# A graph attention layer's aggregation product in seven half-size products instead of eight

## The chip, the cores and the metric

The kernel runs on one core of a Trainium2 chip. The metric is the device time of one execution in microseconds. The times before and after are medians of several runs. The kernel is written so that the order of the instructions on TensorE (PE), VectorE (DVE), ScalarE (ACT) and the SyncE queue that issues the DMAs (SP) is the order in which the program states them, engine by engine; semaphores are set between the engines wherever one needs another's result.

## The reference

For each of 32 batches, with n = 512 nodes and d = 512 features, all in f32:

```
layer 0:  q, k, v = x Wq' + bq, x Wk' + bk, x Wv' + bv        (8 heads of 64)
          a = softmax(q k' / 8 + log(max(adj, 1e-8)))
          y = layer_norm(x + concat(a v) Wo' + bo) * gamma + beta
layer 1:  p = y fc_w' + fc_b
          m = (p q_w + q_b) + (p k_w + k_b)' + (1 - adj) * -1e9
          e = softmax(leaky_relu(m))
          out = e p + y
```

In layer 1 the kernel does not form p. With n the normalised rows ahead of gamma and beta, it computes e n first (with e not yet divided by its row sums), then multiplies by fc with gamma folded in, divides by the row sums and adds gamma n and a constant row, called cc, that holds beta and the bias of the projection. The product e n, stored transposed in a tile named zT, is what is changed.

## The kernel before

A batch b is worked in four slots, one for each pair of heads, p = 0 to 3; I call them the first to the fourth slot. Each slot computes the scores of one pair of heads (`score`, L814, with the exponential at L819), multiplies them by the adjacency (`factors`, L827), adds up their rows (`sums`, L837 and L840) and multiplies by v for the pair before (`values`, L852). Around this, the slots carry work of other batches, written out by hand:

- The first slot of batch b has e n of batch b - 2 (`z`, which calls `z_units`, products at L310, copies out of PSUM at L452). The transposes of e (`eT`, L535) and of the adjacency (`turn_a`, L557) come ahead of it on VectorE; after it come gamma n and the constant row (`residual`, L443 and L444), the reciprocal of the row sums (L437) and `divided`, which checks and inverts softmax sums, stores them with one small DMA (L895) and loads them spread out with two (L898) into a tile R.
- The second slot has the output projection of layer 0 of batch b - 1 (`seven_wo`), its sums on VectorE at L740 and its adds at L744, then the statistics of the layer norm (`stats_units`). It begins with the loads of n and of the next x.
- The third slot normalises (`normalise_units`), takes dot products with the k vector (L376), and does the last projection of batch b - 2 (`seven_out`, called from `layer1_rows`): `z_sums` makes two sums of quarters of zT, one of them in a tile z3; the products are at L205, the sums between them at L761, the adds of the results at L767. The transposes of the next x are among them.
- The fourth slot has v of the next batch (`seven_v`) and the softmax of layer 1 of batch b - 1.

In every slot the next pair's q and k are made by `seven_qk` (L604), as four units; the second, third and fourth end with ScalarE or VectorE work, the adds of the last two at L634, L638 and L639.

All the functions whose names begin with `seven` use Winograd's form of Strassen's method: a 512x512x512 product is cut into quarters, and seven products of quarters, with sums of quarters made on VectorE ahead of them and adds of results behind them, do the work of eight. A product of quarters is four matmuls of 128x128 weights with 256 columns. e n is made in the plain way: 16 matmuls with 512 columns. A matmul of f32 is two records in the trace, so this is 32 records, and a product of quarters 8.

The tiles that matter: n (a batch's normalised rows), eP (transposed e), L1 (holds e's rows early, zT later), yb (gamma n + cc, later the output rows), R (two halves of 512 columns). A pool of three PSUM banks, `ps_m`, serves e n, the W_o and v projections and the last projection.

Of the kernel before, what the change touches and what calls it, by code (L numbers as in the profile page):

```python
# [9 lines left out]
FP = mybir.dt.float32  # L10
# [20 lines left out]
def kernel(  # L31
# [19 lines left out]
    k_b: bass.AP,  # L51
    out: bass.AP,
):

# [381 lines left out]

    def residual(s, cs=slice(0, 4)):

        def over(row):
            return row.unsqueeze(1).to_broadcast([P, cs.stop - cs.start, D])
        nc.vector.tensor_mul(s["yb"][:, cs, :], s["n"][:, cs, :], over(K["gamma"]))  # L443
        nc.vector.tensor_add(s["yb"][:, cs, :], s["yb"][:, cs, :], over(K["cc"]))  # L444

    def z_units(s, psum, name):

# [30 lines left out]
    def fast(ctx):  # L478
# [18 lines left out]

        cT = act.tile([P, NC, N], FP, name="cT")
        L1 = act.tile([P, NC, N], FP, name="L1")

        def load_a(b, kcs):

# [52 lines left out]
        def turn_a(kcs):  # L555
            for kc in kcs:
                nc.vector.transpose(cT[:, kc, :], cT[:, kc, :])  # L557
# [33 lines left out]
        def seven_qk(b, p):  # L591

            qk_tiles(b, p)
            s = S[b]
            q, k = s["qT", p], s["kT", p]
            bq, bk = K["bq"][:, p : p + 1], K["bk"][:, p : p + 1]
            wq, wk, W = K["wq"], K["wk"], K["qk_s"]
            left = {1: wq[:, :KH], 2: wq[:, KH:], 3: W[:, 2], 4: wk[:, KH:],
                    5: W[:, 0], 6: W[:, 1], 7: wk[:, :KH]}
            ps = {}  # L600

            def mul(i, to, first):
                for c in range(KH):
                    nc.tensor.matmul(  # L604
                        to, left[i][:, c, ts(p, P)], s["B"][i][:, c, :],
                        start=(first and c == 0), stop=(c == KH - 1),
                        skip_group_check=True,
                    )

            def banks():  # L610
                f = [ps_s.tile([P, 2, N], FP, tag="s", name=f"f_{b}_{p}_{i}") for i in range(2)]
                for i, name in enumerate("acbd"):
                    ps[name] = f[i % 2][:, i // 2, :H]

            def unit0():
                banks()
                mul(1, ps["a"], True)
                mul(5, ps["c"], True)  # L620
                nc.scalar.copy(ps["b"], ps["a"])  # L621
                nc.scalar.activation(k[:, H:], ps["c"], AF.Identity, bias=bk)

            def unit1():
                mul(6, ps["a"], False)
                mul(2, ps["b"], False)
                nc.scalar.activation(q[:, H:], ps["a"], AF.Identity, bias=bq)  # L627
                nc.scalar.activation(q[:, :H], ps["b"], AF.Identity, bias=bq)

            def unit2():  # L630
                mul(4, ps["d"], True)
                mul(3, ps["c"], False)
                nc.scalar.activation(k[:, :H], ps["d"], AF.Identity, bias=bk, scale=-1.0)  # L633
                nc.vector.tensor_add(q[:, H:], ps["c"], q[:, H:])  # L634

            def unit3():
                mul(7, ps["a"], False)
                nc.vector.tensor_add(k[:, H:], ps["a"], k[:, H:])  # L638
                nc.vector.tensor_add(k[:, :H], ps["a"], k[:, :H])  # L639
            return [unit0, unit1, unit2, unit3]  # L640

        def seven_v(b):

# [105 lines left out]
        def seven_out(b):  # L749

            s = S[b]
            yb, zT, r = s["yb"], s["zT"], s["r"]
            tiles = {
                f"{i + 1}{j + 1}": zT[:, ts(j, KH), ts(i, H)] for i in range(2) for j in range(2)
            }
            tiles["s3"] = s["z3"]
            data = {i: [t[:, c, :] for c in range(KH)] for i, t in tiles.items()}
            ps = {}

            def sub(i, x, y):  # L760
                nc.vector.tensor_sub(tiles[i], tiles[x], tiles[y])  # L761

            def add(i, j, name):
                for c in range(KH):
                    row = i * KH + c
                    o = yb[:, row, ts(j, H)]
                    nc.vector.scalar_tensor_tensor(  # L767
                        o, ps[name][:, c, :], r[:, row : row + 1], o, ALU.mult, ALU.add
                    )

            def store(i):
                nc.sync.dma_start(
                    out=out[b][ts(i, KH * P), :].rearrange("(c p) d -> p c d", p=P),
                    in_=yb[:, ts(i, KH), :],
                )

            def unit0(unit):
                ps.update(zip("bac", long_banks(f"o{b}")()))
                unit(True)
            muls, adds = seven_rows(data, sub, K["fc_s"], K["fc"], lambda n: ps[n], add, True)  # L780
            muls[0] = lambda unit=muls[0]: unit0(unit)
            adds[2].insert(1, lambda: store(0))
            adds[3].append(lambda: store(1))
            return muls, adds

        def z_sums(b):

            s = S[b]
            zT = s["zT"]
            s["z3"] = act.tile([P, KH, H], FP, tag="z3", name=f"z3_{b}")  # L790
            a11, a21, a22 = zT[:, :KH, :H], zT[:, :KH, H:], zT[:, KH:, H:]
            nc.vector.tensor_sub(s["z3"], a11, a21)
            nc.vector.tensor_add(a21, a21, a22)

        def long_banks(b):
# [159 lines left out]
        def z(b):  # L955
            s = S[b]
            s["zT"] = L1
            return z_units(s, ps_m, b)

        def eT(b):  # L960
            s = S[b]
            if b >= B - 2:
                t = io.tile([P, NC, N], FP, tag="x", name=f"eT_{b}")
                s["eT"] = t.rearrange("p t (c n) -> p t c n", c=NC)
                return transpose_units(s["e"], t, ps_m, nc.scalar.copy, f"e_{b}")
            s["eT"] = s["eP"].rearrange("p c (t n) -> p t c n", t=NC)
            return transposes(s["eP"], s["eP"])
# [64 lines left out]
        def slot(b, p):  # L1032
# [38 lines left out]
            if p == 0 and last >= 0:  # L1071
                if b >= 2:
                    run(eT(b - 2))
                turn_a((2, 3))
                divide(last, 2)
            factors(b, p, 1)
            if p == 3 and last >= 0:
                divided(b, 0)
            if p == 2:
# [4 lines left out]
                next_qk = seven_qk(b, p + 1)  # L1084
            else:
                next_qk = seven_qk(nxt, 0)
            if p == 0:
                sums(b, p, 0)
                if b == 0:
                    run(combine(K["wv"], K["v_s"])[:1] + combine_qk()[:1])  # L1090
                run(next_qk)
                units = z(b - 2) if b >= 2 else [lambda: spread(ps_o)] if b == 1 else first_v[2:]
                run(units)
                if b == 1:
                    combine_right(K["fc"], K["fc_s"])
                if b == 0:
                    run(combine(K["wv"], K["v_s"])[1:])
                if b >= 2:
                    rest_of_layer1(b - 2)
                if last >= 0:  # L1100
                    divided(last, 2)
            if p == 1:
                sums(b, 0, 1)
                if last < 0:
                    sums(b, p, 1)
                    run(next_qk)
                    bias()
                else:
                    for i in range(3):
                        wos[i + 1]()  # L1110
                        run(wo_adds[i])
                        if i == 1:
                            sums(b, p, 1)
                        next_qk[i]()
                    next_qk[3]()
                    wos[4]()
                    run(wo_adds[3])
                    run(stats_units(S[last], small, last))
            if p == 2:
                if b == 0:  # L1120
                    combine_right(K["wo"], K["wo_s"])
                    run(next_qk)
                    run(xT(nxt))
                    sums(b, p, 0)
                    offset()
                    divided(b, 0)
                else:
                    return layer1_rows(b, next_qk, norm[1:])
            if p == 3:
                load_a(nxt, (2, 3))  # L1130
                vs = seven_v(nxt)
                vs[0]()
                run(soft[1:2])
                next_qk[0]()
                vs[1]()
                next_qk[1]()
                run(soft[2:])
                sums(b, 2, 1)
                vs[2]()
                next_qk[2]()  # L1140
                next_qk[3]()
                vs[3]()
                turn_a((0, 1))
                sums(b, p, 0)
                sums(b, p, 1)
# [299 lines left out]
```

## Time and profile before

| what | value |
|---|---|
| median of 3 runs | 3474.84 us (3474.70 to 3476.26) |
| the profiled execution's own time | 3475.4 us |
| its span in the profile | 3473.5 us |
| TensorE busy | 3451.6 us, 99% of the span |
| VectorE busy | 2813.1 us, 81% |
| ScalarE busy | 1375.9 us, 40% |
| granted TensorE clock | 0.999 |
| DMA | 250.81 MB, mean 72 GB/s |

The profile has a page of totals and groups, and the trace behind it can be asked for a stretch of time. "Busy" counts the time in which an engine had an instruction running. TensorE's records overlap[...], so the distance from start to start tells more than the length. A row of a timeline gives the start, the length, the engine, the line in the source, the operation, the tile written and those read, the shape, how many instructions were merged into the row, and in brackets how long the engine had been idle before it and what it had waited for. A row of the waits gives who waited for whom, the total, the number of times and the longest.

### The profile page before, as it was taken

Reading aid. Unit: us, or ns where it says so; the run is one execution under the profiler, and the core shown is the slowest. Engines: PE = TensorE matmul, PEld = TensorE weight load, DVE = VectorE, ACT = ScalarE, POOL = GpSimd, SP = SyncE. Lnnn points to the kernel's source line nnn. Section 1 sums busy time; section 2 is a strip of 40 time slices with the busy share of each in tenths; the row PEclk is TensorE's granted clock in tenths of the full one; section 3 lists DMA queues with packets and bytes.
Section 4 is the critical chain, followed back from the end, with each engine's and each line's share of the span. In section 5 each row is a group of like instructions: output and inputs, shape, how many; then the busy total and the mean of one; then the engine's idle time right before and its main releaser. Section 6 shows DMA issues by size and latency. Waiting matters only on the chain.

```text
span 3473.5 us, 40744 instructions
## 1 busy us (share of the span) xinstructions
PE 3451.6 (99%) x14530; PEld 2193.0 (63%) x14530; DVE 2813.1 (81%) x4911; ACT 1375.9 (40%) x2338; POOL 1.0 (0%) x9
## 2 busy tenths in 40 slices
PE   9999999999999999999999999999999999999998
PEld 3666666666666666666666666676666666666654
DVE  5888888788887888788888878888788878888875
ACT  3343443434433444434334333443344343434432
POOL 0000000000000000000000000000000000000000
PEclk9999999999999999999999999999999999999999
DMA  4244243343333442433424334333344243343420
GB/s 116 41 74 89 59 87 66 56 89 78 70 71 57 82 89 59 80 68 62 89 63 84 65 56 89 80 68 73 59 77 89 59 82 65 62 89 65 82 74 31
DMA packets 880025, 250.81 MB, mean 72 GB/s; under 512 B 806732, under 2 KB 806988, under 8 KB 879816
## 3 DMA queue, kind: packets, MB, share of 16 engines
q1 hardware_dynamic: 879816, 248.15, 36.5%
q8 instruction: 116, 1.90, 0.2%
q14 instruction: 93, 0.76, 0.1%
HBM read 181.93 MB, written 34.65 MB: 62 GB/s over the span
## 4 chain that ended last, share of the span: by engine, by line
PE 97%; DVE 2%; DMA 1%; ACT 0%; issue 0%; SPq 0%; DVEq 0%; ACTq 0%
PE f L604 22%; PE sc L814 14%; PE po L852 13%; PE pz L310 12%; PE pw_a L205 6%; PE pv_a L205 5%; PE pw_o_a L205 4%; PE pw_c L205 3%; PE pv_b L205 3%; PE pv_c L205 3%; PE pw_o_b L205 3%; PE pw_o_c L205 3%; PE ps L869 2%; PE pw_b L205 2%; PE pg L310 1%; PE pk L310 0%
## 5 line engine op out<-in xcount | busy, mean ns | idle before, releaser
L827 DVE SCALAR_TENSOR_TENSOR at<-cT,at 128x1024 f32<-128x1024 f32 x512 | 601.1, 1215 | 224.0 <-ACT at L819 220.4
L819 ACT ACTIVATE at<-sc 128x1024 f32<-128x1024 f32 x512 | 496.6, 1022 | 604.2 <-PE sc L814 603.0
L814 PE MATMUL sc<-qT,kT 64*128 64x512 f32 x2048 | 508.8, 615 | 2.2 <-DVE kT L639 2.2
L852 PE MATMUL po<-at,v 128*64 128x512 f32 x2048 | 467.8, 599 | 0.0
L310 PE MATMUL pz<-eP,n 128*128 128x512 f32 x960 | 416.9, 592 | 0.0
L814 PEld LDWEIGHTS sc<-qT,kT 64*128 64x128 f32 x2048 | 176.3, 186 | 283.7 <-issue 283.6
L852 PEld LDWEIGHTS po<-at,v 128*64 128x64 f32 x2048 | 135.5, 136 | 316.6 <-issue 312.9
L310 PEld LDWEIGHTS pz<-eP,n 128*128 128x128 f32 x960 | 182.4, 190 | 216.8 <-issue 215.2
L840 DVE TENSOR_TENSOR as<-as,at 128x1024 f32<-128x1024 f32 x254 | 310.3, 1222 | 5.4
L604 PE MATMUL f<-xT,wq 128*128 128x256 f32 x992 | 261.0, 386 | 0.0
L604 PE MATMUL f<-T,qk_s 128*128 128x256 f32 x992 | 244.6, 379 | 0.0
L452 ACT COPY L<-pz 128x512 f32<-128x512 f32 x128 | 74.9, 586 | 397.9 <-PE pz L310 397.9
L604 PEld LDWEIGHTS f<-xT,wq 128*128 128x128 f32 x992 | 183.4, 190 | 74.4 <-ACT at L819 52.0
L604 PEld LDWEIGHTS f<-T,qk_s 128*128 128x128 f32 x992 | 188.2, 190 | 26.1 <-ACT f L621 0.3
L860 ACT COPY oT<-po 128x512 f32<-128x512 f32 x128 | 75.2, 588 | 289.7 <-PE po L852 289.7
L837 DVE TENSOR_TENSOR as<-at,at 128x1024 f32<-128x1024 f32 x128 | 155.0, 1211 | 1.1
L744 DVE TENSOR_TENSOR n<-pw_a,n 128x512 f32<-128x512 f32 x96 | 66.4, 692 | 98.9 <-PE pw_a L205 98.9
L627 ACT ACTIVATE qT<-f,bq 128x256 f32<-128x256 f32 x124 | 58.3, 470 | 220.2 <-PE f L604 220.2
L633 ACT ACTIVATE kT<-f,bk 128x256 f32<-128x256 f32 x124 | 58.5, 472 | 196.4 <-PE f L604 196.4
L604 PE MATMUL f<-xT,qk_s 128*128 128x256 f32 x496 | 127.3, 379 | 0.0
L604 PE MATMUL f<-xT,wk 128*128 128x256 f32 x496 | 127.3, 379 | 0.0
L604 PE MATMUL f<-T,wk 128*128 128x256 f32 x496 | 127.3, 379 | 0.0
(234 smaller groups left out, 5314.9 us busy)
## 6 DMA issues: line engine op xcount, KB each, us to landing
cT<-in_adj_dram SPq DMA_DIRECT2D x512, 64.0 KB
R<-d SPq DMA_DIRECT2D x126, 256.0 KB
x<-in_x_dram SPq DMA_DIRECT2D x124, 256.0 KB
n<-in_x_dram SPq DMA_DIRECT2D x31, 1024.0 KB
L<-in_adj_dram SPq DMA_DIRECT2D x60, 512.0 KB
eP<-L SPq DMA_DIRECT2D x480, 64.0 KB
out_dram<-yb SPq DMA_DIRECT2D x58, 512.0 KB
w<-dk SPq DMA_DIRECT2D x32, 256.0 KB
```

Source lines behind the costliest of these rows:

```text
L205: nc.tensor.matmul(to[:, n, :], data(i, c)[:, ts(n, P)], weights[i][:, c, :], start=(first and n == 0 and c == 0), stop=(n == KH - 1 and c ...
L310: nc.tensor.matmul(ps, lhs(i), rhs(i), start=(i == 0), stop=(i == 3))
L452: nc.scalar.copy(s["zT"][:, d, :], pz)
L604: nc.tensor.matmul(to, left[i][:, c, ts(p, P)], s["B"][i][:, c, :], start=(first and c == 0), stop=(c == KH - 1), skip_group_check=True,)
L814: nc.tensor.matmul(sc[:, j, :], s["kT", p][rows, ts(kc, P)], s["qT", p][rows, :], start=True, stop=True,)
L819: nc.scalar.activation(at, sc, AF.Exp, scale=SCALE)
L827: nc.vector.scalar_tensor_tensor(at, cT[:, kc, :].unsqueeze(1).to_broadcast([P, 2, N]), ADJ_MIN, at, ALU.max, ALU.mult,)
L837: nc.vector.tensor_add(s["as", p], s["at", p, 0], s["at", p, 1])
L840: nc.vector.tensor_add(s["as", p], s["as", p], s["at", p, kc])
L852: nc.tensor.matmul(s["po", p][j * DK : (j + 1) * DK, :], s["v"][h // 4][:, kc, ts(h % 4, DK)], s["at", p, kc][:, j, :], start=(kc == 0), s ...
L860: nc.scalar.copy(s["oT"][p], s["po", p])
L869: nc.tensor.matmul(ps[h * BL : (h + 1) * BL, :], ones[:, :BL], s["as", p + h // 2][:, h % 2, :], start=True, stop=True,)
```

## The change

1. `z` is replaced, for b >= 2, by `seven_z`: seven products of quarters of n and e. Sums of quarters are made on VectorE, most of them in place of n and e, two into scratch space: s1 into a tile named `third`, t1 into the second half of R of the batch before, which is loaded later. `third` is also used by the last projection in place of z3.
2. Since n is overwritten, gamma n (`scaled`) is taken in two halves ahead of the sums that overwrite it. The constant row (`offset_rows`) and the reciprocal (`invert`) move to the end of the second slot, behind the statistics.
3. `seven_qk` returns five units: the fourth only the last product, the fifth all three adds. In the first slot the first four go ahead of e n, the adds among its steps.
4. In the first slot, the transposes of the adjacency's second half and `factors` of the second half move behind e n's products; `divided` goes ahead of its last product in the order of the program. In the second slot, the second half of the first pair's sums moves from the start to the middle of the W_o projection, and the second pair's from there to one unit later.

The diff, cut to its core:

```diff
+        def seven_z(b):
+            s = S[b]
+            n, e = s["n"], s["eP"]
+            s["zT"] = zT = L1
+            s1 = third
+            t1 = S[b + 1]["R", 2][:, 1, :].rearrange("p (c n) -> p c n", c=KH)
+            A = {f"{i + 1}{j + 1}": n[:, ts(j, KH), ts(i, H)] for i in range(2) for j in range(2)}
+            E = {f"{i + 1}{j + 1}": e[:, ts(j, KH), ts(i, H)] for i in range(2) for j in range(2)}
+            C = {f"{i + 1}{j + 1}": zT[:, ts(i, KH), ts(j, H)] for i in range(2) for j in range(2)}
+            left = {1: A["11"], 2: A["12"], 3: A["12"], 4: A["22"], 5: s1, 6: A["11"], 7: A["21"]}
+            right = {1: E["11"], 2: E["21"], 3: E["22"], 4: E["21"], 5: t1, 6: E["11"], 7: E["12"]}
...
+            def unit0():
+                ps.update(zip("bac", long_banks(f"z{b}")()))
+                mul(1, "a", True)
+                mul(5, "c", True)
+                nc.scalar.copy(ps["b"], ps["a"])
+                nc.scalar.copy(C["22"], ps["c"])
+            def unit1():
+                mul(6, "a")
+                mul(2, "b")
+                nc.scalar.copy(C["12"], ps["a"])
+                nc.scalar.copy(C["11"], ps["b"])
+            def unit2():
+                mul(7, "a")
+                mul(3, "c")
+            def unit3():
+                mul(4, "a")
+                nc.scalar.copy(C["21"], ps["a"])
+            def before0():
+                sub(t1, E["12"], E["11"])
+                nc.vector.tensor_add(s1, A["21"], A["22"])
+            def before1():
+                sub(A["21"], A["11"], A["21"])
+            def after0():
+                sub(E["11"], E["22"], t1)
+                sub(A["11"], s1, A["11"])
+            def after1():
+                sub(E["12"], E["22"], E["12"])
+            def before2():
+                sub(A["12"], A["12"], A["11"])
+                sub(E["21"], E["21"], E["11"])
+            def after2():
+                nc.vector.tensor_add(C["22"], ps["a"], C["22"])
+            def after3():
+                nc.vector.tensor_add(C["12"], ps["c"], C["12"])
...
             if p == 0 and last >= 0:
                 if b >= 2:
                     run(eT(b - 2))
-                turn_a((2, 3))
                 divide(last, 2)
-            factors(b, p, 1)
+                if b == 1:
+                    turn_a((2, 3))
+            if p > 0 or b < 2:
+                factors(b, p, 1)
...
+            if p == 0 and b >= 2:
+                zs, extra = seven_z(b - 2)
+                top, bottom = slice(0, KH), slice(KH, NC)
+                extra[0]()
+                new_yb(b - 2)
+                scaled(S[b - 2], top)
+                extra[1]()
+                run(next_qk[:4])
+                zs[0]()
+                extra[2]()
+                run(next_qk[4:])
+                extra[3]()
+                zs[1]()
+                turn_a((2, 3))
+                scaled(S[b - 2], bottom)
+                extra[4]()
+                zs[2]()
+                extra[5]()
+                divided(last, 2)
+                zs[3]()
+                factors(b, p, 1)
+                extra[6]()
+                sums(b, p, 0)
...
             if p == 1:
-                sums(b, 0, 1)
                 if last < 0:
+                    sums(b, 0, 1)
...
-                        if i == 1:
-                            sums(b, p, 1)
+                        if i > 0:
+                            sums(b, i - 1, 1)
                         next_qk[i]()
-                    next_qk[3]()
+                    run(next_qk[3:])
                     wos[4]()
                     run(wo_adds[3])
                     run(stats_units(S[last], small, last))
+                    if b >= 2:
+                        offset_rows(S[b - 2])
+                        invert(S[b - 2])
```

`extra` is the list of VectorE steps in the order before0, before1, after0, after1, before2, after2, after3.

More of the change, by code (lines that the diff above doesn't have):

```diff
@@ L439, in residual, with over, scaled, offset_rows @@
     def residual(s, cs=slice(0, 4)):
[L441 to L444, printed above, removed]
+        scaled(s, cs)
+        offset_rows(s, cs)
+    def over(row, cs):
+        return row.unsqueeze(1).to_broadcast([P, cs.stop - cs.start, D])
+    def scaled(s, cs):
+        nc.vector.tensor_mul(s["yb"][:, cs, :], s["n"][:, cs, :], over(K["gamma"], cs))
+    def offset_rows(s, cs=slice(0, 4)):
+        nc.vector.tensor_add(s["yb"][:, cs, :], s["yb"][:, cs, :], over(K["cc"], cs))
     def z_units(s, psum, name):
@@ L499, in fast @@
         L1 = act.tile([P, NC, N], FP, name="L1")
+        third = act.tile([P, KH, H], FP, name="third")
         def load_a(b, kcs):
@@ L633, in unit2, with adds @@
                 nc.scalar.activation(k[:, :H], ps["d"], AF.Identity, bias=bk, scale=-1.0)
+            def adds():
                 nc.vector.tensor_add(q[:, H:], ps["c"], q[:, H:])
-            def unit3():
-                mul(7, ps["a"], False)
                 nc.vector.tensor_add(k[:, H:], ps["a"], k[:, H:])
                 nc.vector.tensor_add(k[:, :H], ps["a"], k[:, :H])
-            return [unit0, unit1, unit2, unit3]
+            return [unit0, unit1, unit2, lambda: mul(7, ps["a"], False), adds]
         def seven_v(b):
@@ L755, in seven_out @@
             }
-            tiles["s3"] = s["z3"]
+            tiles["s3"] = third
             data = {i: [t[:, c, :] for c in range(KH)] for i, t in tiles.items()}
@@ L789, in z_sums @@
             zT = s["zT"]
-            s["z3"] = act.tile([P, KH, H], FP, tag="z3", name=f"z3_{b}")
             a11, a21, a22 = zT[:, :KH, :H], zT[:, :KH, H:], zT[:, KH:, H:]
-            nc.vector.tensor_sub(s["z3"], a11, a21)
+            nc.vector.tensor_sub(third, a11, a21)
             nc.vector.tensor_add(a21, a21, a22)
@@ L958, in z, with mul @@
             return z_units(s, ps_m, b)
+        def seven_z(b):
[9 more added lines that the diff above has]
+            right = {1: E["11"], 2: E["21"], 3: E["22"], 4: E["21"], 5: t1, 6: E["11"], 7: E["12"]}
+            ps = {}
+            sub = nc.vector.tensor_sub
+            def mul(i, name, first=False):
+                for m in range(KH):
+                    for t in range(KH):
+                        nc.tensor.matmul(
+                            ps[name][:, m, :].rearrange("p (c n) -> p c n", c=KH),
+                            left[i][:, t, ts(m, P)], right[i][:, :, ts(t, P)],
+                            start=(first and m == 0 and t == 0),
+                            stop=(m == KH - 1 and t == KH - 1), skip_group_check=True,
+                        )
+            def unit0():
[32 more added lines that the diff above has]
+                nc.vector.tensor_add(C["12"], ps["c"], C["12"])
+            return [unit0, unit1, unit2, unit3], [
+                before0, before1, after0, after1, before2, after2, after3
+            ]
@@ L1086, in slot @@
                 next_qk = seven_qk(nxt, 0)
-            if p == 0:
+            if p == 0 and b >= 2:
[21 more added lines that the diff above has]
+                sums(b, p, 0)
+            elif p == 0:
                 sums(b, p, 0)
@@ L1091, in slot @@
                 run(next_qk)
[L1092 to L1095, printed above, removed]
+                run(first_v[2:] if b == 0 else [lambda: spread(ps_o)])
                 if b == 0:
                     run(combine(K["wv"], K["v_s"])[1:])
-                if b >= 2:
-                    rest_of_layer1(b - 2)
-                if last >= 0:
+                else:
+                    combine_right(K["fc"], K["fc_s"])
                     divided(last, 2)
             if p == 1:
-                sums(b, 0, 1)
                 if last < 0:
+                    sums(b, 0, 1)
                     sums(b, p, 1)
@@ L1139, in slot @@
                 vs[2]()
-                next_qk[2]()
-                next_qk[3]()
+                run(next_qk[2:])
                 vs[3]()
```

## The prediction

> **What bounds the kernel now.** I read the page first: busy shares, the chain that ended last, the groups. Then, for one batch in the middle, TensorE's timeline beside VectorE's; a second batch (2380 to 2500 us) has the same waits to 0.01 us.
>
> ```profile
> PE 3451.6 (99%) x14530; PEld 2193.0 (63%) x14530; DVE 2813.1 (81%) x4911; ACT 1375.9 (40%) x2338; POOL 1.0 (0%) x9
> ...
> PE 97%; DVE 2%; DMA 1%; ACT 0%; issue 0%; SPq 0%; DVEq 0%; ACTq 0%
> ...
> L310 PE MATMUL pz<-eP,n 128*128 128x512 f32 x960 | 416.9, 592 | 0.0
> ```
>
> 97% of the chain is TensorE, so a matmul removed is time removed unless TensorE then waits. The third line is the product that is changed: 960 records, 32 in each of 30 batches. Now TensorE's timeline (start, length, what): the seven products of the output projection in the third slot, then e n in the first slot.
>
> ```profile
> 1549.25 1.89 PE L205 MATMUL pw_o_a<-fc_s,L 128*128 128x256 f32 x8
> 1550.98 1.89 PE L205 MATMUL pw_o_c<-fc,L 128*128 128x256 f32 x8
> 1552.76 1.99 PE L205 MATMUL pw_o_a<-fc,z 128*128 128x256 f32 x8
> 1554.59 1.89 PE L205 MATMUL pw_o_b<-fc_s,L 128*128 128x256 f32 x8
> 1556.41 1.99 PE L814 MATMUL sc<-qT,kT 64*128 64x512 f32 x8
> ...
> 1595.86 1.03 PE L604 MATMUL f<-xT,wk 128*128 128x256 f32 x4
> 1596.72 13.90 PE L310 MATMUL pz<-eP,n 128*128 128x512 f32 x32
> 1610.55 1.99 PE L814 MATMUL sc<-qT,kT 64*128 64x512 f32 x8
> ```
>
> Lengths overlap, so I go by starts. e n takes 1610.55 - 1596.72 = 13.83 us. A half-size product takes 1.73 us to the next one (1550.98 - 1549.25), and 1.82 when scores follow. The product at 1552.76 is the only one that comes late: it waits for VectorE.
>
> ```profile
> PEld pw_o_a L205 <- DVE yb L767: 8.6, 29, 0.3
> ```
>
> VectorE's timeline shows where it has room (in brackets the idle time ahead of a row): first slot, then the end of the second and the third.
>
> ```profile
> 1594.86 1.26 DVE L557 STREAM_TRANSPOSE cT<-cT 128x512 f32<-128x512 f32 x2
> ...
> 1602.73 2.29 DVE L444 TENSOR_TENSOR yb<-yb,cc 128x2048 f32<-128x2048 f32 x1
> ...
> 1605.42 0.25 DVE L893 RECIPROCAL c<-c 128x16 f32<-128x16 f32 x1
> 1612.78 2.36 DVE L827 SCALAR_TENSOR_TENSOR at<-cT,at 128x1024 f32<-128x1024 f32 x2 [7.10 <-ACT at L819]
> ```
>
> ```profile
> 1533.43 2.33 DVE L827 SCALAR_TENSOR_TENSOR at<-cT,at 128x1024 f32<-128x1024 f32 x2
> 1536.18 0.16 DVE L358 TENSOR_TENSOR rt<-rstd 128x4 f32<-128x4 f32 x1 [0.42 <-ACT rstd L357]
> ...
> 1547.72 0.88 DVE L767 SCALAR_TENSOR_TENSOR yb<-pw_o_c,r,yb 128x256 f32<-128x256 f32 x2 [0.56 <-PE pw_o_c L205]
> ...
> 1549.45 0.69 DVE L761 TENSOR_TENSOR L<-L 128x512 f32<-128x512 f32 x1 [0.23 <-PE pw_o_b L205]
> ...
> 1551.87 0.83 DVE L767 SCALAR_TENSOR_TENSOR yb<-pw_o_a,r,yb 128x256 f32<-128x256 f32 x2
> ```
>
> In the first slot VectorE stands 7.10 us. In the third it has only 0.42 + 0.56 + 0.23 = 1.21 us between the statistics and the add at 1551.87, which ends at 1552.70 and lets the late product start.
>
> **What the Trainium skill says.** (1) "TensorE: Matmul & The Clock Gate", section "Wait — 56ns, not 53.3ns?": warm matmuls of N columns follow each other by N / 2.4 GHz + 2.5 ns. If each f32 record streams its columns twice, that estimates 215.8 ns for 256 and 429.2 for 512. The trace agrees: 1.728/8 = 216 ns, and 429 between records of e n. (2) Same page, "Architectural detail": TensorE pulls weight loads ahead of running matmuls, VectorE is strictly in order. The trace agrees: weights at 1550.76 for the product at 1550.98. So weights must be ready 0.22 us early, and one late VectorE step delays all behind it. (3) "VectorE: DVE Perf Modes", "The perf-mode tier table": an f32 tensor_tensor runs at 1x, from PSUM too; 2293 ns for 2048 elements. The trace has 2292.
>
> **The change, part by part** (first-slot clock: 0 is 1582.16, the slot's first score).
>
> *Matmuls.* 13.83 us become six products of 1.728 and one of 1.82: 12.19. Saved: 1.64 us x 30 = **49.3 us**. The reordering ahead of it leaves the 28 Q/K records first, so e n still begins at 14.56.
>
> *VectorE, first slot.* Added: eight sums of 512 elements (SBUF) and two adds from PSUM; nearest rows L761 0.69 and L744 0.69, back to back 0.61. gamma n stays (two halves, 1.22 each); the constant row (2.29) and the reciprocal leave. VectorE ends the e transposes at 12.70 (where 1594.86 stands). Then t1, s1 to 13.9; half of gamma n to 15.1; A21 to 15.7. The next pair overwrites operands of product 1, so it waits for that: 14.56 + 1.73 + 0.16 drain + 0.04 = 16.49, a reserve of 0.77. The pair ends at 17.78. Product 6 is due at 18.02, its weights at 17.80: just met, behind product 5. Not shown before is this hand-over's latency: from 0 to 0.3 us a batch; no gain, since nothing there was waiting. I take 0.1: **+3 us**. Then Q/K adds to 18.8, E12 19.4, transposes 20.6, gamma n 21.7, A12 22.4 (product 3's weights due 22.98), E21 23.0, add from product 7 at 23.4 to 24.0 (product 4 due 24.93), the `divided` steps to 24.6, `factors` 26.9, last add 27.5, sums 28.6. The next slot's first `factors` can start 26.75 + 2.23 = 28.98, so all this fits in the former idle time; without that, each us would be a us a batch. Values of the second half need `factors` at 30.4, have it at 26.9.
>
> *Other queues.* ScalarE makes five copies of 0.59 for four; each has a product of 1.73 beside it. `divided` issues one small store and two R loads on SP, still ahead of the n load. Before: arithmetic over 1605.67, R issued from 1607.13, traffic gone by about 1611.3, used at 1616.32. After: issued at about 26.1, landed at 30.3, used at 32.5. SP then reaches the n load at 27.5, 0.75 into the second slot (0.1 before); n is first added 11.2 in, and VectorE may be some 3 us late there. Cost 0; if this cover were gone, the second slot's sum and product 5 of the W_o projection would wait for R. The persistent scratch for the old per-batch one: 0.
>
> *Second slot.* The first sums (2.40) move behind the first set of W_o adds and push the second sums back, behind the add that ended at 22.15 of this slot. These end at 24.55, the K adds at 25.66; the third slot's score needs K at 25.75. Cost 0 to 0.2; I take 0 (0.09 left). At the slot's end come the constant row and reciprocal: 1605.03 - 1602.73 = 2.30 us. Behind them on VectorE: the third slot's `factors`, rstd, sums, k dots, Q/K adds, output sums and adds. The wait of 0.42 (rstd is there), 0.56 and 0.23 vanish, with 0.07 of overlap regained at each: 2.30 - 1.21 - 0.21 = 0.88 late at the add of 1551.87. Its product waits already, so TensorE stops by all of it: 0.88 x 29 = **+25.5 us** (batch 31 has another output path, where VectorE waits 1.81). Bounds 0.7 to 1.2. Behind it VectorE waits for TensorE again (0.52 at 1554.80), so nothing carries over.
>
> *Sum.* -49.3 + 25.5 + 3 = -20.8. The profiled execution took 3475.4 (span 3473.5 and 1.9 around it): 3454.6. The median shown is 0.56 lower: 3454.0.
>
> **Rivals.** *B, nothing given back.* The third slot's lateness is absorbed, for instance since its adds overlap more than I count: -49.3, so 3425.5. For: VectorE is busy 81% only. Against: the 8.6 us row, 29 waits out of 29 at just that add. *C, hand-overs cost more.* First-slot pair and third-slot score each 0.25 to 0.3 us late on top: 0.5 x 30 = 15 more, about 3469. For: margins of 0.02 and 0.09. Against: VectorE started 0.04 after a matmul's end and TensorE 0.06 after VectorE's in the rows used. *D, slower: the added sums are dearer.* Place: products 1 to 6. With d us for a sum, three lie ahead of product 1's end (reserve 0.77), two behind it, so TensorE stands 5(d - 0.69) - 0.77 a batch; from d = 1.0 this eats the net gain of 0.75. At d = 1.28, 2.2 us: about 3474.8 - 20.8 + 63 = 3517. For: the moving operand and sums are quarters cut in rows and columns. Against: L761 works on such quarters in 0.69. That dependencies are taken by whole tiles (product 1 then waits for A21) belongs here too; against it, L761 wrote a quarter of L at 1546.48 while TensorE read another.
>
> **How the numbers follow.** Likeliest 0.70: 3454, own range 3446 to 3469 (-49.3, 29 times 0.7 to 1.2, 30 times 0 to 0.3, a little air). B 0.12, C 0.11, D 0.07. A range of 3440 to 3471 leaves out B and D, 0.19. What can be told from no change is 0.2%, 7 us: below 3467.9 lie the likeliest, B and a little of C, 0.84; C's rest 0.09 is within; D 0.07 slower.
>
> **What would show it.** e n at 216 ns a record, 12.2 us from its first to the next score; the first slot's wait of 7.10 nearly gone; in the third slot the row of weights waiting for yb from 0.3 to about 1.2 us each, the rstd wait gone. Wrong would be: gaps inside e n over 0.3 us (D), or the third slot's projection still at 12.3 us (B).

## The result and the profile after

The changed kernel takes 3442.47 us (median of 4 runs, 3441.04 to 3444.82); the kernel before took 3475.55 beside it. The ratio is 0.9906, 95% interval 0.9888 to 0.9923: 33.1 us less, where 20.8 were forecast. The time lies 3.5 us below the range of the likeliest course (3446 to 3469) and 2.5 us above the lower end of the whole range (3440 to 3471). The span went from 3473.5 to 3440.3, 33.2 less, so the trace can account for all of it.

First the page of the kernel after: busy shares, the chain, and the group of the new products into bank a.

```profile
PE 3407.7 (99%) x15250; PEld 2329.9 (68%) x15250; DVE 2992.5 (87%) x5241; ACT 1391.0 (40%) x2368; POOL 0.9 (0%) x9
...
PE 84%; DVE 11%; ACT 3%; issue 1%; DMA 0%; DVEq 0%; SPq 0%; ACTq 0%
...
L986 PE MATMUL pw_z_a<-eP,n 128*128 128x256 f32 x960 | 226.9, 379 | 0.4 <-DVE n L1023 0.4
```

TensorE is as full as before, VectorE went from 81% to 87%. The chain now runs over VectorE for 11% instead of 2%: some stretch is now set by VectorE's work. It isn't e n: the products into bank a, four of the seven, waited 0.4 us in the whole execution. TensorE's timeline of one batch shows e n:

```profile
1584.38 1.89 PE L986 MATMUL pw_z_a<-eP,n 128*128 128x256 f32 x8
1586.10 1.89 PE L986 MATMUL pw_z_c<-R,third 128*128 128x256 f32 x8
1587.83 1.89 PE L986 MATMUL pw_z_a<-eP,n 128*128 128x256 f32 x8
...
1594.74 1.89 PE L986 MATMUL pw_z_a<-eP,n 128*128 128x256 f32 x8
1596.56 1.99 PE L821 MATMUL sc<-qT,kT 64*128 64x512 f32 x8
```

From the first product to the next score it is 1596.56 - 1584.38 = 12.18 us (13.83 before), with 1.73 from each product to the next: no gap. The third slot's projection is where time is lost:

```profile
1536.36 1.89 PE L206 MATMUL pw_o_a<-fc_s,L 128*128 128x256 f32 x8
1538.09 1.89 PE L206 MATMUL pw_o_c<-fc,L 128*128 128x256 f32 x8
1540.42 1.99 PE L206 MATMUL pw_o_a<-fc,third 128*128 128x256 f32 x8 [0.44 <-DVE yb L775]
1542.25 1.89 PE L206 MATMUL pw_o_b<-fc_s,L 128*128 128x256 f32 x8
1544.07 1.99 PE L821 MATMUL sc<-qT,kT 64*128 64x512 f32 x8
```

Without a wait the last product would start two products, 3.455 us, after 1538.09, at 1541.55. It starts at 1542.25, so 0.70 us are lost; before it was 1554.59 - 1550.98 - 3.455 = 0.16. The loss grew by 0.54 us in 29 batches, 15.7 us. The rows of waits say the same. A wait in these rows is the engine's idle time and not the time lost (here 0.44 for the product and 0.84 for its weights, where 0.70 were lost), so I compare the rows of before and after:

```profile
PE pw_o_a L206 <- DVE yb L775: 12.6, 29, 0.4
...
PEld pw_o_a L206 <- DVE yb L775: 24.2, 29, 0.8
```

The weights' wait was 8.6 and is 24.2: 15.6 more. And VectorE, first slot, then the end of the second and the third:

```profile
1585.09 0.69 DVE L1019 TENSOR_TENSOR n<-n 128x512 f32<-128x512 f32 x1
1586.31 0.69 DVE L1022 TENSOR_TENSOR eP<-eP,R 128x512 f32<-128x512 f32 x1 [0.52 <-PE pw_z_a L986]
1586.91 0.69 DVE L1023 TENSOR_TENSOR n<-third,n 128x512 f32<-128x512 f32 x1
...
1598.79 2.36 DVE L834 SCALAR_TENSOR_TENSOR at<-cT,at 128x1024 f32<-128x1024 f32 x2 [0.29 <-ACT at L826]
```

```profile
1520.53 2.26 DVE L452 TENSOR_TENSOR yb<-yb,cc 128x2048 f32<-128x2048 f32 x1
...
1525.03 0.16 DVE L359 TENSOR_TENSOR rt<-rstd 128x4 f32<-128x4 f32 x1
...
1525.82 0.16 DVE L363 SCALAR_TENSOR_TENSOR rt<-mv,rstd 128x4 f32<-128x4 f32 x1
1525.90 2.35 DVE L834 SCALAR_TENSOR_TENSOR at<-cT,at 128x1024 f32<-128x1024 f32 x2
...
1535.74 0.87 DVE L775 SCALAR_TENSOR_TENSOR yb<-pw_o_c,r,yb 128x256 f32<-128x256 f32 x2
...
1539.53 0.83 DVE L775 SCALAR_TENSOR_TENSOR yb<-pw_o_a,r,yb 128x256 f32<-128x256 f32 x2
```

In the first slot the wait of 7.10 is down to 0.29, and the pair that waits for product 1 has 0.52 us to spare. In the third slot none of the three waits of before (0.42, 0.56, 0.23) is left, and the add that frees bank a for the late product comes at 1539.53.

The account: 30 x (13.83 - 12.18) = 49.5 saved, 15.7 given back in the third slot, and 0.02 a batch at the second slot's last score (1.84 us after the product ahead of it, 1.82 before), 0.6: 33.2. Starts are read to 0.01 us, so each term over 30 batches can be off by some tenths of a us, and that the sum meets the span to the tenth is luck.

### The profile page after: what moved, and what is told of

Read it like the earlier page. It is cut to its first block, busy times and chain, and to the rows that moved or that the text cites. A ratio compares the mean times of both kernels' runs of the same rounds, so it can differ in the third digit from the quotient of the medians.

```text
span 3440.3 us, 42725 instructions
## 1 busy us (share of the span) xinstructions
PE 3407.7 (99%) x15250; PEld 2329.9 (68%) x15250; DVE 2992.5 (87%) x5241; ACT 1391.0 (40%) x2368; POOL 0.9 (0%) x9
## 4 chain that ended last, share of the span: by engine, by line
PE 84%; DVE 11%; ACT 3%; issue 1%; DMA 0%; DVEq 0%; SPq 0%; ACTq 0%
PE f L613 18%; PE sc L821 14%; PE po L859 13%; PE pw_a L206 6%; PE pw_z_a L986 6%; PE pv_a L206 5%; PE pw_c L206 3%; PE pv_b L206 3%; PE pv_c L206 3%; PE pw_z_c L986 3%; ACT n L367 2%; DVE xT L544 2%; DVE R L377 2%; PE pw_o_a L206 2%; PE ps L876 2%; PE pw_b L206 2%
## 5 line engine op out<-in xcount | busy, mean ns | idle before, releaser
L986 PE MATMUL pw_z_a<-eP,n 128*128 128x256 f32 x960 | 226.9, 379 | 0.4 <-DVE n L1023 0.4
L986 PEld LDWEIGHTS pw_z_a<-eP,n 128*128 128x128 f32 x960 | 180.2, 190 | 27.7 <-issue 0.9
L206 PE MATMUL pv_a<-wv,xT 128*128 128x256 f32 x496 | 120.4, 386 | 0.0
```

The lines of the kernel that those rows point to most:

```text
L206: nc.tensor.matmul(to[:, n, :], data(i, c)[:, ts(n, P)], weights[i][:, c, :], start=(first and n == 0 and c == 0), stop=(n == KH - 1 and c ...
L986: nc.tensor.matmul(ps[name][:, m, :].rearrange("p (c n) -> p c n", c=KH), left[i][:, t, ts(m, P)], right[i][:, :, ts(t, P)], start=(first ...
```

## The experiments

My theory: TensorE sets the time; e n's saving is whole; what is given back is VectorE work put ahead of one add in the third slot, less those of VectorE's waits there that lie behind it and ahead of the add. The rivals: the third slot is late for another reason that comes with the change; the first slot's load is what is paid for; or work on VectorE costs TensorE its whole length. Each result below is a median in us and its ratio to the kernel before, run beside it (3476.04 for the first four, 3475.85 for the last three), with the 95% interval of the ratio.

**The constant row in the second slot's gap.** VectorE has a wait of 2.33 us there, behind the first set of W_o adds.

```diff
...
                         run(wo_adds[i])
+                        if i == 0 and b >= 2:
+                            offset_rows(S[b - 2])
+                            invert(S[b - 2])
...
                     run(stats_units(S[last], small, last))
-                    if b >= 2:
-                        offset_rows(S[b - 2])
-                        invert(S[b - 2])
```

> The changed kernel with the constant row and the reciprocal moved from the end of the second slot into the gap of 2.33 us that VectorE has there behind the first set of W_o adds. My theory: the row at the slot's end is what makes the seventh-product wait of the third slot's projection grow by 0.54 us in 29 batches, so 15.7 us go: 3442.5 - 15.7 = 3426.8, and the product starts 3.50 us after the one ahead of the one before it, as in the kernel before the change. Rival, that the wait grew for another reason (the halves of gamma n, the five-unit Q/K products, more use of SBUF): the time stays at 3442, the wait at 0.8 us.

Measured: 3426.71, ratio 0.9858 (0.9843 to 0.9873). The row of waits is back where it was before the change, and so is the chain:

```profile
PE 97%; DVE 1%; DMA 1%; ACT 0%; issue 0%; SPq 0%; DVEq 0%; ACTq 0%
...
PEld pw_o_a L206 <- DVE yb L775: 8.6, 29, 0.3
```

The growth of the wait came from the row's place. This kernel also isolates the products: with nothing more lost in the third slot, the change is worth 49.3 us (44 to 55 by the interval), as worked out.

**The other part alone: e n in the plain way, only the row moved to the end of the second slot.**

```diff
...
                 if b >= 2:
-                    rest_of_layer1(b - 2)
+                    new_yb(b - 2)
+                    residual(S[b - 2], add=False)
...
                     run(stats_units(S[last], small, last))
+                    if b >= 2:
+                        offset_rows(S[b - 2])
+                        invert(S[b - 2])
```

> The kernel before the change, e n by eight products in the plain way, with only the constant row and the reciprocal moved to the end of the second slot. My theory: the matmuls are those of before, and the third slot's projection waits 0.54 us more in 29 batches: 3475.5 + 15.7 = 3491. Rival, that the first slot's VectorE load is what the third slot pays for: 3475.5, as VectorE still has 7 us to spare there.

Measured: 3493.17, ratio 1.0051 (1.0037 to 1.0065), 17.1 us more. Two rows of its waits:

```profile
DVE at L833 <- ACT at L825: 292.4, 35, 9.5
...
PEld pw_o_a L205 <- DVE yb L773: 24.6, 29, 1.0
```

The first slot's VectorE load was lighter than before: the row has left it and no sums have come, and the long wait there is 9.5 us instead of 7.1. The third slot's wait has grown all the same (24.6), so the first slot's load is not what it pays for. The two parts add up: -49.3 and +17.1 give -32.2, and both together -33.1.

**The row back in the first slot.**

```diff
                 extra[6]()
                 sums(b, p, 0)
+                offset_rows(S[b - 2])
+                invert(S[b - 2])
```

(The same two calls are taken out of the second slot.)

> The changed kernel with the constant row and the reciprocal put back at the end of the first slot. My theory: VectorE has 0.29 us left there, so the second slot's start comes 2.26 - 0.29 = 1.97 us late on VectorE; the first sums over halves of oT end at 1.97 after 1604.28, that is 0.6 us too late for the second product of the W_o projection, 30 times 0.62 = 18.6 us lost, and the third slot's 15.7 won back: about 3445.4. Rival, that the former idle time of 7 us still has room: the 15.7 come back and nothing is lost, 3427.

Measured: 3434.50, ratio 0.9883 (0.9868 to 0.9898). The third slot's row of waits is back at 8.6. There is a loss against the first experiment's 3426.7, so the first slot is full; but it is 7.8 us, not 18.6. The two intervals just overlap, but the runs do not (3425.8 to 3429.4 there, 3433.0 to 3437.9 here). VectorE's and TensorE's timelines of this kernel show why the loss is small:

```profile
1600.85 0.75 DVE L928 TENSOR_TENSOR oT<-oT,oT 128x256 f32<-128x256 f32 x2
```

```profile
1599.40 1.99 PE L206 MATMUL pw_a<-wo,oT 128*128 128x256 f32 x8
1601.41 1.97 PE L206 MATMUL pw_c<-wo_s,oT 128*128 128x256 f32 x8
1603.21 1.03 PE L613 MATMUL f<-xT,wq 128*128 128x256 f32 x4
```

The row at 1600.85 is two instructions of 0.42 us, one for each half of the operand. The product's first weight load comes from the first half, ready a third of a microsecond ahead of the end of both, and starts at 1601.38; both halves end at 1601.60. In the changed kernel it starts 1.61 us after the product ahead does (1605.59 - 1603.98), here 1.98, so 0.37 late. The product behind starts at 1603.21 and not at 1599.40 + 1.83 + 1.73 = 1602.96: 0.25 us late, 30 times, 7.5. I had let the product wait for both halves, and had not taken off the 0.11 us or so by which weights may be late (last section).

**Two sums ahead of product 1's end made twice.**

```diff
                 extra[0]()
+                extra[0]()
                 new_yb(b - 2)
```

> The changed kernel with the two sums t1 and s1 each made twice, which changes no result. It makes VectorE 1.3 us later ahead of the pair that waits for e n's first product. My theory: it had 0.52 us to spare and so starts 0.7 late; the weights of product 6 come 0.75 later than it can take them, some 0.11 of which is hidden: 0.64 x 30 = 19 us lost, 3461.7, all inside e n. Rival, that the product behind (1.73 us) or the reordered queue hides it: 3442.5. Rival, that sums cost TensorE their whole length: 1.3 x 30 = 39, 3481.

Measured: 3461.46, ratio 0.9957 (0.9943 to 0.9971), 19.0 us more than the changed kernel.

```profile
1593.96 1.89 PE L986 MATMUL pw_z_c<-R,third 128*128 128x256 f32 x8
1596.19 1.97 PE L986 MATMUL pw_z_a<-eP,n 128*128 128x256 f32 x8 [0.34 <-DVE n L1023]
1597.99 1.89 PE L986 MATMUL pw_z_b<-eP,n 128*128 128x256 f32 x8
```

The product behind comes at 1597.99 and not at 1593.96 + 3.455 = 1597.42: 0.57 us, 17 in 30 batches. The hand-over in e n is thus real, with half a microsecond of reserve as the change stands. Work on VectorE doesn't cost TensorE its whole length (3481 by that rival), and it isn't hidden either (3442.5).

**One transpose fewer in the chain that is left.** On top of the first experiment's kernel:

```diff
-            run(muls[:1] + adds[0])
             turns = xT(nxt)
-            run(turns[:1] + muls[1:2] + adds[1][:1] + turns[1:])
+            run(muls[:1] + adds[0][:1] + turns[:1] + adds[0][1:])
+            run(turns[1:2] + muls[1:2] + adds[1][:1] + turns[2:])
```

> The changed kernel with the constant row in the second slot's gap, and in the third slot one of the three x transposes behind the sum of quarters moved ahead of it, into VectorE's wait for the projection's second product. My theory: what is left of the third slot's stop, 0.16 us a batch beyond a product's 1.73, is VectorE's chain of that sum, three transposes and two adds; with one transpose (0.6 us) fewer in it the stop goes, 0.16 x 29 = 4.6 us: 3426.7 - 4.6 = 3422.1. Rival, that the 0.16 is the price of the switch of operands and no wait: 3426.7.

Measured: 3420.69, ratio 0.9839 (0.9826 to 0.9853): faster than both kernels, and the fastest here; 6.0 us below the first experiment where 4.6 were expected, which the intervals leave room for. In its timeline the projection no longer stops:

```profile
1527.51 1.89 PE L206 MATMUL pw_o_c<-fc,L 128*128 128x256 f32 x8
1529.23 1.89 PE L206 MATMUL pw_o_a<-fc,third 128*128 128x256 f32 x8
1530.96 1.89 PE L206 MATMUL pw_o_b<-fc_s,L 128*128 128x256 f32 x8
```

**Two sums of the third slot moved to the second, the row left where the change put it.** `z_sums` is called between the sum and the adds of the W_o projection's second set instead of in the third slot.

```diff
...
-                        run(wo_adds[i])
+                        run(wo_adds[i][:1])
+                        if i == 1 and 2 <= b < B - 1:
+                            z_sums(b - 2)
+                        run(wo_adds[i][1:])
...
             if b >= 2 and nxt < B:
-                z_sums(b - 2)
```

> The changed kernel, its constant row still at the end of the second slot, with the two sums of quarters of zT (1.33 us on VectorE) taken out of the third slot and made in VectorE's wait of 1.37 us in the second. My theory: what delays the third slot is the amount of VectorE work ahead of that add, not the row as such; 1.33 less takes away all of the 0.54, but not the 0.16 that was there before, since the sum behind the second product then waits for TensorE again: 3442.5 - 15.7 = 3426.8. Rival, that the row delays TensorE by itself, by what is queued directly behind it: 3442.

Measured: 3428.92, ratio 0.9863 (0.9848 to 0.9878). The wait is 8.6 us again. It is the amount of work ahead of the add that counts, not the row.

**One sum of the third slot made three times, the row in the gap.**

```diff
-            nc.vector.tensor_sub(third, a11, a21)
+            for _ in range(3):
+                nc.vector.tensor_sub(third, a11, a21)
```

> The changed kernel with the constant row in the second slot's gap, and in the third slot the first of the two sums of quarters of zT made three times, which changes no result: 1.44 us more of VectorE work, put in behind the first of VectorE's waits there. My theory: the two waits behind it (0.56 and 0.23, with 0.07 of regained overlap at each) take 0.93 of it, so TensorE stops 0.5 longer in 29 batches: 3426.7 + 14.8 = 3441. Rival, that all waits of the slot count, whatever their place (1.7 us): 3426.7. Rival, that none does: 1.44 x 29 = 42, 3468.

Measured: 3441.38, ratio 0.9897 (0.9882 to 0.9912), 14.7 more than without the repeats. The waits of this kernel, and below them the last of these rows in the changed kernel, show which of VectorE's waits was left:

```profile
PEld pw_o_a L206 <- DVE yb L775: 21.9, 29, 1.0
...
DVE rt L359 <- ACT rstd L358: 14.2, 32, 0.6
```

```profile
DVE rt L359 <- ACT rstd L358: 1.0, 2, 0.6
```

The wait for rstd, ahead of the added work, stays at 14.2 us; in the changed kernel, where the row lay ahead of it, it is 1.0. Only waits behind the added work absorb it. The rivals of this run, that all waits count (3426.7) or that none does (3468), both fail.

## Why the prediction was right, and by how much it was off

*The matmuls.* Right: 12.19 forecast, 12.18 measured, and 49.3 us shown by the first experiment.

*VectorE in the first slot.* Right in order and nearly in time. On the first-slot clock the pair was to end at 17.78 and ended at 1587.60 - 1569.82 = 17.78; its reserve was 0.52 instead of 0.77, in part since the sums ahead of it began 0.1 later. The 3 us for the hand-over were not needed: the weights of product 6 came 0.11 us late and the product did not. The prediction asked for weights 0.22 us ahead of their product; here 0.11 was enough. Nor did rival C's further 0.5 us a batch at the hand-overs appear: e n has no gap, and the third slot's score comes 0.02 later behind its product. Rival D's place was the right one to watch, as the doubled sums show, but the sums cost 0.69, as the nearest row said.

*Other queues.* R was to be issued at 26.1 and used at 32.5: 26.2 and 32.5 in the trace. The first n add still waits for TensorE and not for the load.

*Second slot.* 0 forecast, 0.02 a batch measured.

*Third slot.* The mechanism was right, its size was not: 0.88 us late at the add, 25.5 us in all, against 0.54 and 15.7, below the bounds of 0.7 to 1.2 that I had set. The term that failed is what VectorE's waits absorb. From the score that begins the third slot, the add came at 22.36 before (1551.87 - 1529.51) and comes at 22.91 after (1539.53 - 1516.62), 0.55 later for the 2.26 that row and reciprocal take from start to start (I had 2.30). So 1.71 were absorbed, where I had counted 1.21 + 0.21 = 1.42. The largest missing piece is a wait that carries no bracket in the timeline: from the first of the five small rstd steps to the next `factors` it took 1536.18 to 1537.24 before, 1.06 us, and 1525.03 to 1525.90 after, 0.87. Before, `factors` had to wait for its exponential, which started at 1536.18 and takes 1.02; it ended at 1537.20. That is 0.19. The other runs agree: this stretch takes 0.87 where the row lies ahead of it (second and sixth experiments) and 1.06 where it does not (first and seventh). The remaining 0.10 is spread over overlaps of a few hundredths; I haven't tried to settle it. Rival B's claim, that more is absorbed than I counted, thus held in part; it did not hold that all of it is.

Together: 9.8 us too much for the third slot and 2.4 too much for hand-overs make up the difference of 12 to the measured gain. Both errors point the same way, so neither hid the other.

## What to carry to other kernels

When the bound engine loses work and a second engine gains some, write the second engine's queue out from the trace, with each start, and look for the one hand-over where it is already late; the gain elsewhere is kept only as far as that hand-over allows. Waits absorb added work only if they lie behind it and ahead of the hand-over, and start-to-start distances, with the gaps too short to be reported as waits, give what they absorb better than the sum of reported idle times. A step without a due time, like this constant row, belongs in a gap whose end is set by the bound engine: the same 2.26 us cost 15.7 us at the slot's end, 7.8 in a full slot, and nothing in a gap of 2.33.

## What the runs showed of the hardware that I had not expected

- Weights that came 0.11 us later than without a wait cost no matmul time: product 6's loads start at 1587.72, where 1585.89 + 1.73 = 1587.62 was due, and the product starts on time at 1587.83. Beyond that, lateness costs: 0.37 us late cost 0.25 in the third experiment, 0.68 late cost 0.57 in the fourth.

```profile
1585.89 1.70 PEld L986 LDWEIGHTS pw_z_c<-R,third 128*128 128x128 f32 x8
1587.72 1.60 PEld L986 LDWEIGHTS pw_z_a<-eP,n 128*128 128x128 f32 x8
```

- In this kernel a product did not wait for the whole of its operand: in the third experiment its first weight load starts at 1601.38, ahead of the end of the second half's sum at 1601.60. With the sum of both halves 1.9 us later, TensorE lost 0.25 us instead of the 0.6 worked out for the whole operand.
- A 256-column f32 product whose moving operand is two pieces of 128 columns from different chunks runs at the same 216 ns a record (1.73 us for eight, the new products of e n) as one with contiguous columns (the last projection's products).
